# Seeding four LSTM steps at once from 32 stationary columns, with the state in zeroed 32-column tiles

## The chip, the cores and the metric

The kernel runs on one core of a Trainium2 chip. The metric is the device time of one execution in microseconds (us), lower is better; a time is the median of several executions. The profile is one further execution, recorded by the hardware profiler. Engines: PE (TensorE, matmul), with its weight loads shown apart as PEld; DVE (VectorE); ACT (ScalarE); POOL (GpSimd); SP, which issues DMAs.

## The reference, cut to what matters

Two layers on x of shape (8, 512, 256). The part that the change touches is an LSTM over the 512 positions, batch 8, input and state of 256 features; after it come routed attention heads that need all its outputs and their mean over time.

```python
xw = x @ Wx + b                          # (8, 512, 1024), four gates of 256
for t in range(512):
    i, f, o, g = split(xw[:, t] + h @ Wh)    # h: (8, 256)
    c = sigmoid(f) * c + sigmoid(i) * tanh(g)
    h = sigmoid(o) * tanh(c)
```

Step t needs h of step t - 1: the 512 steps are a chain.

## The kernel before, in words

The stages follow each other: a Nystrom attention with an edge sum, the LSTM (`lstm`, lines 598 to 712), routed heads, the second layer's attention, and an RNN with experts. In the LSTM stage the order on PE, ACT and DVE is written out by hand (`manual_schedule`): each engine runs its instructions in the order of the program. POOL and SP are not in that list.

*A step.* The gates' values for all of a step lie in PSUM with the batch on partitions: the 1024 columns are four quarters j of 256, and quarter j goes to partitions 32 j to 32 j + 7, so that each quarter uses its own 32-column tile of PE's array. Of each quarter, 128 columns go to `pgi` (gates i and f), 64 to `pgg`, 64 to `pgo` (function `parts`). For each of these three and each half k of the state, line 677 issues four matmuls, j = 0 to 3, with the state `hp` of 128 x 8 as the stationary operand and a piece of `wh` as the moving one. A float32 matmul appears as two records in the profile, so pgi's 8 matmuls are 16 records.

*The chain.* DVE transposes pgi in 32 x 32 blocks into `G` (line 683), ACT takes tanh (684), the same follows for pgg and pgo (687, 688; the sigmoids are written with tanh, and the weights are scaled for it). DVE forms the products (690, 691) and the new c (693), ACT takes its tanh (695), and DVE writes the state of the step into `ring` (696), a tile of 8 steps. Line 677 of the next step reads it there. X, `to` and `th` are tiles of a pool with three buffers, `ring` of one with two.

*Seeds.* Before its recurrent matmuls, each PSUM tile holds the input share xw + b of its step. `seed` (line 657) puts it there with a matmul of its own: eight columns of the identity, those of the step's batch rows in `xw`, are stationary, and a piece of `xw` is moving. Per step these are 12 matmuls, three per quarter. pgi has two buffers and its seeds for step t + 1 follow the recurrent matmuls of step t directly; pgg and pgo have one, and their seeds stand at the end of step t, after the background pieces, and wait until DVE has transposed the old values.

*Background pieces.* Work that is not part of the chain is cut into generators, of which a step takes a piece after its state is written:
- `project` makes xw for the next 16 steps: two POOL copies, then four matmuls of 128 x 512 moving columns (line 643) and four DVE additions (line 647, 256 columns each), one a step from t % 16 = 7 on: matmuls at 7 to 10, additions at 11 to 14.
- `rest` is the gating of the layer's input, 16 positions at a time in 7 pieces: (1) four matmuls into pv (line 533) and two additions on DVE (535); (2) two ACT operations that read pv (538) and two DVE operations (539); (3) a product (542); (4) a tanh on ACT (544) and, once it is done, a DVE operation (545); (5) a square on ACT (547); (6) a product (549); (7) two additions (552). They stand at t % 16 = 0 to 6.
- `extra` is `adaptive_weights`: 16 rounds of two matmuls with 512 moving columns (line 1065) and an addition with a store (line 1068), at t % 16 = 13 to 15; they end in the first half of the stage.

After each 8 steps DVE sums the ring over time into `hpart` (line 708), and POOL writes half of it to hT, in one instruction (line 709).

Of the kernel before, what the change touches and what calls it, by code (L numbers as in the profile page):

```python
# [18 lines left out]
P = 128  # L19
B = 8  # L20
# [488 lines left out]
def l0_attention(K, es, states):  # L509


    nc, tc, inp = K.nc, K.tc, K.inp
    xT = K.xT
    mm = nc.tensor.matmul
    dp = K.pool(es, "a_d")
    denseT = dp.tile([P, 2, B, S], F32, name="denseT")
    xgT = dp.tile([P, 2, S], F32, name="xgT")
    alpha = dp.tile([P, S], F32, name="alpha")
    wvw = dp.tile([P, 2, D], F32, name="wvw")
    nc.sync.dma_start(out=wvw, in_=inp["wv_w"].rearrange("(k p) n -> p k n", p=P))  # L520

    def gating(gp, pp):


        TT, STT = nc.vector.tensor_tensor, nc.vector.scalar_tensor_tensor
        for t in range(0, S, GT):
            ts = slice(t, t + GT)
            d, x = denseT[:, :, :, ts], xT[:, :, :, ts]
            e, v, sg = [gp.tile([P, 2, B, GT], F32, name=n, tag=n) for n in ("e", "v", "sg")]
            pv = pp.tile([P, 2, B * GT], F32, name="pv", tag="pv")  # L530
            for dc in range(2):
                for k in range(2):
                    mm(pv[:, dc], wvw[:, k, dc * P : (dc + 1) * P], d[:, k], start=(k == 0), stop=(k == 1))
            for dc in range(2):
                TT(e[:, dc], d[:, dc], xgT[:, dc, ts].unsqueeze(1).to_broadcast([P, B, GT]), ALU.add)
            yield
            for dc in range(2):
                nc.scalar.activation(v[:, dc].rearrange("p b t -> p (b t)"), pv[:, dc], AF.Identity, bias=K.cols[:, 2 + dc : 3 + dc])
                STT(x[:, dc], e[:, dc], 2.0, x[:, dc], ALU.mult, ALU.add)
            yield  # L540
            v2, e2, sg2 = [w.rearrange("p k b t -> p (k b) t") for w in (v, e, sg)]
            TT(v2, v2, alpha[:, ts].unsqueeze(1).to_broadcast([P, 16, GT]), ALU.mult)
            yield
            nc.scalar.activation(sg2, v2, AF.Tanh)
            STT(v2, e2, -0.5, v2, ALU.mult, ALU.add)
            yield
            nc.scalar.activation(sg2, sg2, AF.Square, bias=K.ones[:, 0:1], scale=-1.0)
            yield
            TT(v2, v2, sg2, ALU.mult)
            yield  # L550
            for dc in range(2):
                TT(x[:, dc], x[:, dc], v[:, dc], ALU.add)
            yield

    with ExitStack() as e1:
        dr = K.pool(e1, "a_dram", 1, DRAM)
        gp = K.pool(es, "a_g", 2)
        edges = Edges(K, e1, dr)
        with tc.tile_pool(name="n_pre", bufs=1) as pool:
            nystrom(K, modulated(K, pool, dr, denseT), denseT, xgT)  # L560
        hT, lw = states()
        rest = gating(gp, K.pool(es, "a_pv", 1, PSUM))
        with ExitStack() as e2:
            enc0 = K.pool(e2, "a_wv").tile([P, 2, S], F32, name="enc0")
            nc.vector.tensor_tensor(enc0, denseT[:, :, 0, :], xgT, ALU.add)
            with tc.manual_schedule(engines=ORDERED):
                for g, _ in enumerate(edges.sums(enc0, e2, alpha)):
                    if g == 1:
                        weights = lstm_weights(K, lw)
                    if g in (4, 6):  # L570
                        next(rest)
    for _ in range(5):
        next(rest)
    return hT, rest, weights
# [23 lines left out]
def lstm(K, hT, rest, weights, extra):  # L598
# [15 lines left out]
    with ExitStack() as es:  # L614
        wp = K.pool(es, "l_w")
        sp = K.pool(es, "l_s", 3)
        rp = K.pool(es, "l_r", 2)
        xp = K.pool(es, "l_xw", 2)
        psx = K.pool(es, "l_px", 1, PSUM)
        psg = K.pool(es, "l_pg", 1, PSUM)  # L620
        wx, wh, bias = weights
        h0 = wp.tile([P, 2, B], F32, name="h0")
        nc.vector.tensor_scalar(h0, K.h0T, 2.0, None, ALU.mult)
        pick = ident.rearrange("p (b t) -> p t b", b=B)

        pgi = [psg.tile([P, 2, 64], F32, name=f"pgi{i}") for i in range(2)]
        pgg, pgo = [psg.tile([P, 64], F32, name=n) for n in ("pgg", "pgo")]
        for t in (*pgi, pgg, pgo):
            nc.vector.memset(t, 0.0)
        X = sp.tile([P, 4, 2, B], F32, name="X", tag="X")  # L630
        nc.vector.memset(X[:, 3], 0.0)

        def project(t0):

            xw = xp.tile([P, 1024], F32, name="xw", tag="xw")
            px = psx.tile([P, 1024], F32, name="px", tag="px")
            xc = xp.tile([P, 2, P], F32, name="xc", tag="xc")
            for k in range(2):
                nc.gpsimd.tensor_copy(xc[:, k].rearrange("p (b t) -> p b t", b=B), xT[:, k, :, t0 : t0 + XB])
            yield xw  # L640
            for n in range(2):
                for k in range(2):
                    mm(px[:, n * 512 : n * 512 + 512], xc[:, k], wx[:, k, n * 512 : n * 512 + 512], start=(k == 0), stop=(k == 1))
                    yield
            for n in range(4):
                c = slice(n * 256, n * 256 + 256)
                nc.vector.tensor_tensor(xw[:, c], px[:, c], bias[:, c], ALU.add)  # L647
                yield

        def parts(t):  # L650

            return (pgi[t % 2], 0, 128), (pgg, 128, 192), (pgo, 192, 256)

        def seed(t, xw, part):
            for dst, lo, hi in part:
                for j in range(4):
                    mm(dst[32 * j : 32 * j + B], pick[:, t % XB, :], xw[:, j * 256 + lo : j * 256 + hi], start=True, stop=False)  # L657

        proj = project(0)
        xw = next(proj)  # L660
# [1 line left out]
            pass  # L662
        proj = iter(())
        nxt = None
        ring = None
        seed(0, xw, parts(0))
        E = mybir.EngineType
        es.enter_context(K.tc.manual_schedule(engines={E.PE, E.Activation, E.DVE}))
        for t in range(S):
            if t % RB == 0:  # L670
                last = ring
                ring = rp.tile([P, RB, 2, B], F32, name="ring", tag="ring")
            for dst, lo, hi in parts(t):
                for k in range(2):
                    hp = h0[:, k, :] if t == 0 else (ring[:, t % RB - 1, k] if t % RB else last[:, RB - 1, k])
                    for j in range(4):
                        mm(dst[32 * j : 32 * j + B], hp, wh[:, k, j * 256 + lo : j * 256 + hi], start=False, stop=(k == 1))  # L677
            if t + 1 < S:
                if t % XB == XB - 1:
                    xw = nxt  # L680
                seed(t + 1, xw, parts(t + 1)[:1])
            G = sp.tile([P, 4, 2, 32], F32, name="G", tag="G")
            nc.vector.transpose(G[:, 0:2].rearrange("p g k b -> p (g k b)"), pgi[t % 2].rearrange("p g n -> p (g n)"))  # L683
            nc.scalar.activation(X[:, 0:2], G[:, 0:2, :, 0:B], AF.Tanh)  # L684
            to = sp.tile([P, 2, B], F32, name="to", tag="to")
            for g, ps, th in ((2, pgg, X[:, 2]), (3, pgo, to)):
                nc.vector.transpose(G[:, g].rearrange("p k b -> p (k b)"), ps)
                nc.scalar.activation(th, G[:, g, :, 0:B], AF.Tanh)
            pr = sp.tile([P, 2, 2, B], F32, name="pr", tag="pr")
            STT(pr[:, 1], X[:, 1], 1.0, X[:, 3], ALU.add, ALU.mult)  # L690
            STT(pr[:, 0], X[:, 0], 1.0, X[:, 2], ALU.add, ALU.mult)
# [1 line left out]
            STT(X[:, 3], pr[:, 1], 0.5, pr[:, 0], ALU.mult, ALU.add)  # L693
            th = sp.tile([P, 2, B], F32, name="th", tag="th")
            nc.scalar.activation(th, X[:, 3], AF.Tanh, scale=0.5)  # L695
            STT(ring[:, t % RB], to, 1.0, th, ALU.add, ALU.mult)  # L696
            if t % XB == 7 and t - 7 + XB < S:
                proj = project(t - 7 + XB)
                nxt = next(proj)
            next(proj, None)  # L700
            if t % XB < 7:
                next(rest, None)
            if t % XB > 12:
                next(extra, None)
            if t + 1 < S:
                seed(t + 1, xw, parts(t + 1)[1:])
            if t % RB == RB - 1:
                nc.vector.tensor_reduce(K.hpart[:, t // RB], ring.rearrange("p t k b -> p k b t"), AX.X, ALU.add)
                nc.gpsimd.tensor_scalar(
                    hT[:, :, :, t - RB + 1 : t + 1], ring.rearrange("p t k b -> p k b t"), 0.5, None, ALU.mult  # L710
                )
        for _ in extra:
            pass

# [28 lines left out]
def routed_heads(K, hT, T):  # L747
# [4 lines left out]
    with ExitStack() as es:  # L752
# [18 lines left out]
        for k in range(2):  # L771
            mm(pl, hsum[:, k, :], wr[:, k, :], start=(k == 0), stop=(k == 1))
        lg = wp.tile([B, NH], F32, name="lg")
        nc.vector.scalar_tensor_tensor(lg, pl, 0.5 / S, br, ALU.mult, ALU.add)
        nm = wp.tile([B, 1], F32, name="nm")
        sm = wp.tile([B, 1], F32, name="sm")
        nc.vector.tensor_reduce(nm, lg, AX.X, ALU.max, negate=True)
# [272 lines left out]
def adaptive_weights(K, wd, hT):  # L1050
# [2 lines left out]
    mm = nc.tensor.matmul  # L1053
    with ExitStack() as es:
        sp = K.pool(es, "d_s", 2)
        ps = K.pool(es, "d_ps", 1, PSUM)
        for n in range(16):
            c = slice(n * S, (n + 1) * S)
            w2 = sp.tile([P, 2, S], F32, name="w2")
            nc.sync.dma_start(out=w2, in_=inp["ada_w2"][:, c].rearrange("(k p) n -> p k n", p=P))  # L1060
            b2 = sp.tile([B, S], F32, name="b2")
            nc.sync.dma_start(out=b2, in_=inp["ada_b2"][c].partition_broadcast(B))
            pw = ps.tile([B, S], F32, name="pw", tag="ps")
            for k in range(2):
                mm(pw, hT[:, k, :], w2[:, k, :], start=(k == 0), stop=(k == 1))
                yield
# [891 lines left out]
```

## Time and profile before

| | us |
|---|---|
| median of 10 executions (4143.86 to 4151.25) | 4147.59 |
| the profiled execution, its own time | 4140.28 |
| its span, first to last instruction | 4138.5 |
| LSTM stage in it, line 677 first to line 696 last | 457.5 to 1711.6 |

Busy in the whole span: PE 86%, PEld 55%, DVE 58%, ACT 35%, POOL 15%. A line of the costliest groups is read thus: line, engine, operation, what it writes and reads, the shape (128x64 is partitions x elements; "128*8" is the stationary operand), the count, then busy time in us, mean duration in ns, and the idle time of the engine just before with what ended most of it. In a timeline the first column is the start in us, the second the time from the first start to the last end of the instructions that the line merges. Durations of matmuls include their way through the array; how fast they follow each other is seen from their starts.

### The profile page before, as it was taken

The numbers are of one execution on the slowest core, as the hardware profiler recorded it, in microseconds if no ns is written. First come the engines' busy times: TensorE is split into PE (matmuls) and PEld (weight loads), VectorE is DVE, ScalarE is ACT, GpSimd is POOL, SyncE is SP. The second block draws the span as 40 slices with busy tenths as digits, with TensorE's granted clock in tenths as the row PEclk, the third lists the DMA queues.
The fourth block names the chain that finished last, engine by engine and source line by source line (L and its number), as shares of the span: only waits on it lengthen the run. The fifth ranks groups of instructions, "written<-read, shape, count | busy, mean of one in ns | idle before, by whom it ended". The sixth has DMA issues, their size and how long they took to land.

```text
span 4138.5 us, 150218 instructions
## 1 busy us (share of the span) xinstructions
PE 3561.6 (86%) x64484; PEld 2280.7 (55%) x64484; DVE 2396.6 (58%) x8916; ACT 1462.7 (35%) x5391; POOL 605.6 (15%) x1250
## 2 busy tenths in 40 slices
PE   8899888888888888699989899889899798989784
PEld 5533455555555555366545555555555465666563
DVE  4488666666666666466666766766766433333232
ACT  3111233333333333255444444534444222333242
POOL 1010000000000000111022222222222111121312
PEclk9899999999999999899999999999999998999798
DMA  2121000000000000200000000000000302443376
GB/s 104 42 72 67 18 20 15 21 20 15 5 4 4 4 4 17 69 17 24 2 1 1 1 2 1 2 1 1 1 1 1 105 3 94 127 130 107 103 233 212
DMA packets 104844, 173.11 MB, mean 42 GB/s; under 512 B 12576, under 2 KB 71872, under 8 KB 103792
## 3 DMA queue, kind: packets, MB, share of 16 engines
q1 hardware_dynamic: 79792, 114.23, 9.2%
q0 software_dynamic: 12064, 34.34, 2.6%
q10 hardware_dynamic: 12320, 14.94, 1.0%
q8 instruction: 505, 8.27, 0.9%
q14 instruction: 163, 1.34, 0.1%
HBM read 124.53 MB, written 40.10 MB: 40 GB/s over the span
## 4 chain that ended last, share of the span: by engine, by line
PE 43%; DVE 9%; ACT 3%; DMA 2%; issue 2%; SPq 0%; ACTq 0%; POOL 0%; POOLq 0%; DVEq 0%; another core or an unknown queue 0%
PE pg L1375 5%; PE pp L1166 4%; PE pe L1202 4%; DVE sm L1218 3%; PE pt L1241 3%; PE pg L1597 3%; PE po L1257 3%; PE px L1276 3%; PE pe L893 2%; DMA x<-xs 2%; PE pp L869 1%; PE pt L913 1%; PE pv L1186 1%; PE py L1613 1%; PE pg L1359 1%
## 5 line engine op out<-in xcount | busy, mean ns | idle before, releaser
L677 PE MATMUL pgi<-wh,ring 128*8 128x128 f32 x8176 | 319.3, 274 | 214.2 <-DVE ring L696 211.7
L1222 ACT ACTIVATE sm<-sm,nm 128x388 f32<-128x388 f32 (+3 forms) x512 | 283.0, 554 | 345.8 <-DVE nm L1218 345.7
L1380 DVE STREAM_TRANSPOSE ring<-h 128x64 f32<-128x64 f32 x512 | 125.6, 245 | 435.7 <-ACT h L1379 417.6
L684 ACT ACTIVATE X<-G 128x32 f32<-128x32 f32 x512 | 117.1, 229 | 680.2 <-DVE G L683 680.2
L677 PEld LDWEIGHTS pgi<-wh,ring 128*8 128x8 f32 x8176 | 177.2, 89 | 278.4 <-DVE ring L696 277.3
L1241 PE MATMUL pt<-ident,sm 128*128 128x128 f32 x1280 | 214.6, 284 | 104.5 <-ACT eT L1243 55.8
L683 DVE STREAM_TRANSPOSE G<-pgi 128x128 f32<-128x128 f32 x512 | 161.7, 316 | 245.3 <-PE pgi L677 245.3
L1375 PE MATMUL pg<-wh,ring 128*8 128x64 f32 x8176 | 224.8, 232 | 81.2 <-DVE ring L1380 67.8
L1379 ACT ACTIVATE h<-pg 128x64 f32<-128x64 f32 x512 | 114.2, 223 | 494.5 <-PE pg L1375 434.9
L1241 PEld LDWEIGHTS pt<-ident,sm 128*128 128x128 f32 x1280 | 144.2, 141 | 224.7 <-DVE eT L1243 85.7
L1166 PE MATMUL pp<-hn,wqkv 128*128 128x512 f32 x512 | 247.0, 610 | 5.0 <-DVE hn L1151 5.0
L1232 POOL COPY pme<-sm 128x4 f32<-128x4 f32 x512 | 119.5, 233 | 819.8 <-DVE sm L1231 815.5
L1375 PEld LDWEIGHTS pg<-wh,ring 128*8 128x8 f32 x8176 | 124.6, 92 | 193.7 <-DVE ring L1380 152.2
L677 PE MATMUL pgg<-wh,ring 128*8 128x64 f32 x8176 | 208.7, 219 | 1.6 <-issue 1.6
L677 PE MATMUL pgo<-wh,ring 128*8 128x64 f32 x8176 | 209.2, 219 | 0.2
L657 PE MATMUL pgi<-xw,ident 128*8 128x128 f32 x4096 | 207.9, 273 | 0.5 <-DVE xw L647 0.5
L1218 DVE CUSTOM_DVE_ANT_0 sm<-pe,mask 128x260 f32<-128x260 f32 (+2 forms) x384 | 141.7, 425 | 108.5 <-PE pe L1202 104.7
L696 DVE SCALAR_TENSOR_TENSOR ring<-to,th 128x16 f32<-128x16 f32 x512 | 89.7, 175 | 174.5 <-ACT th L695 174.5
L1243 ACT COPY eT<-pt 128x128 f32<-128x128 f32 (+3 forms) x256 | 108.3, 423 | 215.3 <-PE pt L1241 215.2
L1231 DVE TENSOR_SCALAR sm<-sm,rc 128x388 f32<-128x388 f32 (+3 forms) x512 | 177.3, 389 | 9.1
L1597 PE MATMUL pg<-xT,w 128*128 128x128 f32 x992 | 170.6, 297 | 12.7 <-DVE a L1460 8.9
L657 PEld LDWEIGHTS pgg<-xw,ident 128*8 128x8 f32 x4096 | 73.8, 97 | 186.4 <-DVE X L693 93.3
(503 smaller groups left out, 7994.5 us busy)
## 6 DMA issues: line engine op xcount, KB each, us to landing
w<-in_experts_dram SPq DMA_DIRECT2D x124, 384.0 KB
cb<-order POOLq DMA_DIRECT2D x32, 512.0 KB
x<-xs SPq DMA_DIRECT2D x124, 128.0 KB
ys<-y SPq DMA_DIRECT2D x124, 128.0 KB
xs<-zero ACTq DMA_DIRECT2D x2, 4736.0 KB
w<-in_ada_w_dram SPq DMA_DIRECT2D x16, 512.0 KB
w<-in_moh_w_dram SPq DMA_DIRECT2D x32, 192.0 KB
out_dram<-acc SPq DMA_DIRECT2D x32, 128.0 KB
```

Of the source, the lines that this page charges most:

```text
L657: mm(dst[32 * j : 32 * j + B], pick[:, t % XB, :], xw[:, j * 256 + lo : j * 256 + hi], start=True, stop=False)
L677: mm(dst[32 * j : 32 * j + B], hp, wh[:, k, j * 256 + lo : j * 256 + hi], start=False, stop=(k == 1))
L683: nc.vector.transpose(G[:, 0:2].rearrange("p g k b -> p (g k b)"), pgi[t % 2].rearrange("p g n -> p (g n)"))
L1166: mm(pp, T.wqkv[:, k, 0 : 2048].rearrange("p (i g h n) -> p i g h n", i=2, g=4, h=2)[:, i, g, h], self.hn[b][:, k, :], start=(k == 0), sto ...
L1202: mm(pe[a][:, 0 : w - lo], q[r, h, at], k[r, h, lo:w], start=(h == 0), stop=(h == 1))
L1218: nc.vector.tensor_tensor_reduce(out=sm[a][:, lo:w], in0=pe[a][:, 0 : w - lo], in1=T.mask[:, S - n + lo : 4 + S], scale=-1.0 / 8.0, scalar ...
L1222: nc.scalar.activation(sm[a][:, 0:w], sm[a][:, 0:w], AF.Exp, bias=nm[:, a : a + 1], scale=-1.0, accum_out=su[:, a : a + 1])
L1231: nc.vector.tensor_scalar(sm[a][:, 0:w], sm[a][:, 0:w], rc[:, a : a + 1], None, ALU.mult)
L1241: nc.tensor.transpose(pt[:, j, :], sm[a][:, 4 + j * P : 4 + (j + 1) * P], K.ident)
L1375: mm(pg[32 * j : 32 * j + B], hp, M.wh[:, k, 64 * j : 64 * j + 64], start=False, stop=(k == 1))
L1380: M.pace = nc.vector.transpose(M.ring[:, at].rearrange("p k b -> p (k b)"), h)
L1597: mm(pg, W[m][:, k * D + g * P : k * D + (g + 1) * P], X[m][:, k, :], start=(k == 0), stop=(k == 1))
```

## The change

- The PSUM tiles become two sets of pgi, pgg and pgo. A set now holds four consecutive steps (t = 1 to 4, 5 to 8, ...): step t uses rows 8 ((t + 3) % 4) and on of each quarter's 32 partitions. The seeds of a group of four steps are one matmul per quarter and PSUM tile, with 32 identity columns as the stationary operand (`Picks`); where the four steps lie in two projections (the group that begins at t % 16 = 13), they are two matmuls.
- The group's seeds are issued one quarter j per step, during the four steps of the group before, directly after the state is written: three matmuls a step instead of twelve, or six at t % 16 = 9 to 12.
- The state goes into 8 of 32 columns of a ring slot, the other 24 stay zero, and line 677's stationary operand is 128 x 32: the other steps' rows get zero added. The two rings are fixed tiles, zeroed ahead.
- Two shared PSUM banks (`K.px`) serve the gating's pv, the projection's px (now two tiles of 512 columns) and the adaptive weights' pw; each had its own.
- Pieces move: projection from t % 16 = 4 (matmuls at 4, 5, 8, 9; additions at 6, 7, 10, 11); gating at 9 to 15, one piece out of step (2 to 7 at 9 to 14, the next block's 1 at 15), and two pieces a step in steps 0 to 3; adaptive weights at 0 to 2.
- `hpart` is summed from hT instead of the ring, two steps into the next eight; POOL writes hT in four instructions instead of one.

```diff
+        h0 = wp.tile([P, 2, 32], F32, name="h0")
+        rings = [wp.tile([P, RB, 2, 32], F32, name=f"ring{i}") for i in range(2)]
+        banks = [[psg.tile([P, w], F32, name=f"{n}{i}") for n, w in (("pgi", 128), ("pgg", 64), ("pgo", 64))] for i in range(2)]
...
         def parts(t):
-            return (pgi[t % 2], 0, 128), (pgg, 128, 192), (pgo, 192, 256)
-        def seed(t, xw, part):
-            for dst, lo, hi in part:
-                for j in range(4):
-                    mm(dst[32 * j : 32 * j + B], pick[:, t % XB, :], xw[:, j * 256 + lo : j * 256 + hi], start=True, stop=False)
+            return zip(banks[(t + 3) // 4 % 2], (0, 128, 192), (128, 192, 256))
+        def seed(t, j, xw, nxt):
+            for dst, lo, hi in parts(t):
+                at = slice(j * 256 + lo, j * 256 + hi)
+                pick.seed(dst[32 * j : 32 * j + 32], t, xw[:, at], nxt[:, at] if nxt is not None else None)
...
+        for j in range(4):
+            seed(0, j, xw, xw)
+        for j in range(4):
+            seed(1, j, xw, None)
...
-                        mm(dst[32 * j : 32 * j + B], hp, wh[:, k, j * 256 + lo : j * 256 + hi], start=False, stop=(k == 1))
-            if t + 1 < S:
-                if t % XB == XB - 1:
-                    xw = nxt
-                seed(t + 1, xw, parts(t + 1)[:1])
+                        mm(dst[32 * j : 32 * j + 32], hp, wh[:, k, j * 256 + lo : j * 256 + hi], start=False, stop=(k == 1), skip_group_check=True)
...
-            STT(ring[:, t % RB], to, 1.0, th, ALU.add, ALU.mult)
-            if t % XB == 7 and t - 7 + XB < S:
-                proj = project(t - 7 + XB)
+            STT(ring[:, t % RB, :, 8 * (t % 4) : 8 * (t % 4) + 8], to, 1.0, th, ALU.add, ALU.mult)
+            if 0 < t <= S - 4:
+                ahead = (t + 3) // 4 * 4 + 1
+                seed(ahead, (t + 3) % 4, xw, nxt)
+                if t % XB == 12:
+                    xw, nxt = nxt, None
+            if t % XB == 4 and t - 4 + XB < S:
+                proj = project(t - 4 + XB)
                 nxt = next(proj)
             next(proj, None)
-            if t % XB < 7:
+            for _ in range(2 if t < 4 else t % XB > 8):
                 next(rest, None)
-            if t % XB > 12:
+            if t % XB < 3:
                 next(extra, None)
-            if t + 1 < S:
-                seed(t + 1, xw, parts(t + 1)[1:])
+            if t % RB == 2 and t > RB:
+                total(t // RB - 1)
             if t % RB == RB - 1:
-                nc.vector.tensor_reduce(K.hpart[:, t // RB], ring.rearrange("p t k b -> p k b t"), AX.X, ALU.add)
...
+                for i in range(4):
+                    nc.gpsimd.tensor_scalar(
+                        hT[:, :, :, t - RB + 1 + i : t + 1 : 4],
+                        ring[:, i : RB : 4, :, 8 * i : 8 * i + 8].rearrange("p q k b -> p k b q"),
+                        0.5, None, ALU.mult,
+                    )
...
+class Picks:
+    def seed(self, dst, t, xw, nxt):
+        at = t % 16
+        if at == 0:
+            self.mm(dst, self.ends[:, 1], nxt, start=True, stop=False, skip_group_check=True)
+        elif at == 13:
+            self.mm(dst, self.ends[:, 0], xw, start=True, stop=False, skip_group_check=True)
+            if nxt is not None:
+                self.mm(dst, self.ends[:, 1], nxt, start=False, stop=False, skip_group_check=True)
+        else:
+            self.mm(dst, self.steps[:, at : at + 4, :].rearrange("p t b -> p (t b)"), xw, start=True, stop=False, skip_group_check=True)
```

## The prediction

> **What bounds the kernel now.** The change lies in the LSTM stage, so I first cut the execution by stage (busy time of each engine in stretches): the stage runs from 457 to 1712 us, PE is busy 1037 of these 1255 us, DVE 809, ACT 434, and the granted clock is 1.00. 83% busy doesn't say that PE sets the pace, so the next view is who waited for whom, here from 500 to 1700 us (waiter, releaser: us in total, times, longest).
>
> ```profile
> ACT X L684 <- DVE G L683: 641.8, 490, 2.3
> DVE G L683 <- PE pgi L677: 233.0, 475, 1.2
> PE pgi L677 <- DVE ring L696: 203.3, 313, 0.9
> ```
>
> Everybody waits for everybody in turn: a ring of dependences. The timeline of one quiet step (t % 16 = 12; start, length, engine, line, what):
>
> ```profile
> 1348.24 0.17 DVE L696 SCALAR_TENSOR_TENSOR ring<-to,th 128x16 f32<-128x16 f32 x1 [0.34 <-ACT th L695]
> ...
> 1348.47 0.62 PE L677 MATMUL pgi<-wh,ring 128*8 128x128 f32 x16 [0.68 <-DVE ring L696]
> ...
> 1348.91 0.41 PE L677 MATMUL pgg<-wh,ring 128*8 128x64 f32 x16
> ...
> 1349.14 0.41 PE L677 MATMUL pgo<-wh,ring 128*8 128x64 f32 x16
> 1349.17 0.32 DVE L683 STREAM_TRANSPOSE G<-pgi 128x128 f32<-128x128 f32 x1 [0.41 <-PE pgi L677]
> ...
> 1349.36 0.40 PE L657 MATMUL pgi<-xw,ident 128*8 128x128 f32 x8
> ...
> 1350.67 0.18 DVE L696 SCALAR_TENSOR_TENSOR ring<-to,th 128x16 f32<-128x16 f32 x1 [0.34 <-ACT th L695]
> ```
>
> State written, pgi's 16 matmuls, transpose, tanh, three small DVE operations, tanh, state: 2.43 us. PE idles 0.68 us before line 677: in a quiet step the seeds (line 657) lie beside the chain and cost nothing. They cost only where a background piece makes PE late. Here is t % 16 = 8, with a projection piece:
>
> ```profile
> 1339.42 0.40 PE L657 MATMUL pgi<-xw,ident 128*8 128x128 f32 x8
> ...
> 1339.75 1.12 PE L643 MATMUL px<-wx,xc 128*128 128x512 f32 x2
> ...
> 1340.80 0.18 DVE L696 SCALAR_TENSOR_TENSOR ring<-to,th 128x16 f32<-128x16 f32 x1 [0.41 <-ACT th L695]
> 1340.81 0.30 PE L657 MATMUL pgg<-xw,ident 128*8 128x64 f32 x8
> ...
> 1340.93 0.29 PE L657 MATMUL pgo<-xw,ident 128*8 128x64 f32 x8
> ...
> 1341.04 0.29 PE L677 MATMUL pgi<-wh,ring 128*8 128x128 f32 x4
> ```
>
> The last seeds still run when the state is ready. From the ends of line 696, t = 256 to 479, the sixteen steps take, from t % 16 = 0: 2495, 2467, 2426, 2425, three of 2346, 2425, 2572, 2437, 2502, 2505, four of 2425 ns, sum 38.99 us. Without disturbance: 13 x 2425 + 3 x 2346 = 38.56. The other 429 ns are 244 for projection, 42 for gating's matmuls, and 2 x 71 where line 696 starts a new ring tile (idle 0.41 before it, not 0.34: the view of that line lists 62 separate wait instructions). **So the most that freeing PE and this wait can bring is 0.43 x 32 = 13.7 us.** The three short steps are those in which no separate wait stands before ACT's lines 684, 688 and 695 (418 such waits on 512 executions of line 684); they follow the gating's tanh and square, whose spacing the change keeps, so three remain.
>
> **The change, part by part.** *Seeds.* Today's 12 matmuls (24 records) run on four column tiles side by side: 0.22 for pgi, 0.11 for pgg, 0.11 for pgo, 0.44 us. The new 3 matmuls all go to one column tile, j, and can't stand side by side. What that costs is seen once in this trace, ahead of step 0, where the scheduler emitted the seeds quarter by quarter:
>
> ```profile
> 456.24 0.39 PE L657 MATMUL pgi<-xw,ident 128*8 128x128 f32 x2 [0.52 <-DVE xw L647]
> ...
> 456.46 0.28 PE L657 MATMUL pgg<-xw,ident 128*8 128x64 f32 x2
> ...
> 456.57 0.28 PE L657 MATMUL pgi<-xw,ident 128*8 128x128 f32 x1
> 456.58 0.28 PE L657 MATMUL pgo<-xw,ident 128*8 128x64 f32 x2
> ```
>
> 0.22 from pgi to pgg, 0.11 to pgo, pgo as long: one quarter takes 0.44 us, as the four do together. **PE's time for seeds doesn't fall.** At t % 16 = 9 to 12 the group straddles two projections and each seed is two matmuls: 0.88 us.
>
> *PE's own step length.* Recurrent 0.89 (first record to the next kind) + seeds 0.44 + projection 1.17 (gap, two halves of 0.43, load, gap until the next tiled matmul) = 2.51 us as measured today (2507); the order inside changes, not the sum. The chain becomes 2425 + 20 (below) = 2445, so a projection step makes the next late by some 65. The projection's matmuls move to t % 16 = 4, 5, 8 and 9; 9 has the double seeds: 65 + 442 = 507. Together 3 x 65 + 507 = 702 against 244: +458 ns, in 31 groups **+14.2 us**. Gating's matmuls go to 15: PE 2.54 us, +94 against 42 (today the ring's wait of 71 covers part): **+1.6**. Adaptive pieces (to 0, 1, 2) are column-tiled too and take 0.86 without gaps: 0.89 + 0.44 + 0.86 is under 2.445, nothing. Their weights' loads are issued at 446 us, ten before step 0; SP's stores only move.
>
> *Loads of 32 columns for 8.* Not in the trace; nearest are 8 (line 677) and 64 (here lines 255, 64 moving columns, and 928, 128):
>
> ```profile
> 127.07 0.69 PE L255 MATMUL pkv<-v,e3T 128*64 128x64 f32 x16
> ...
> 1764.54 0.85 PEld L928 LDWEIGHTS po<-eT,v 128*64 128x64 f32 x16 [0.76 <-issue]
> ```
>
> Start by start, the first matmul of such a group is 48 to 50 ns longer than the later ones, with 8 columns 4; afterwards line 928's rounds come every 109 ns as line 677's do, and line 255's every 58.5 against 56. So only the first load shows: (49 - 4) x 24/56 = 20 ns a step, **+10.2 us** (ends 0 and 45 ns: 0 and 23 us).
> The Trainium skill (TensorE: Matmul & The Clock Gate, Part 3, The mechanism) says that a load overlaps running matmuls only when its row group differs; here all have all 128 rows, so by it each of pgi's four rounds would show its load, some 4 x 20 = 80 ns a step and 41 us. The 109 ns rounds of line 928 speak against that, and I go by them.
>
> *DVE.* hpart's reduce (0.37, line 708) moves from after step 7 to after step 2 of eight, last in DVE's queue. At t % 16 = 10 it stands behind a projection addition (0.42, line 647) and a gating product (0.42, line 542), and the next transpose behind all three. Such operations follow each other 0.08 before the last one's end: DVE is free some 0.89 after the state, the transpose could start at 0.77: 0.12 x 31 = **+3.7**. At 2 it stands behind line 1068 (0.67), sixteen times, as it did at 15: nothing. The other moved gating pieces meet no second one. The reduce now waits for POOL's copies, three steps old: free.
>
> *The ring's wait.* The ring tiles are no longer handed back, and the reduce over hT, before each reuse, has already waited for POOL: 62 x 0.071 = **-4.4**. If instead each of POOL's four copies were waited for by the state that overwrites it, it would be 256 x 0.071 - 4.4 = +14; I take the first.
>
> *Start, end, rest.* Second group seeded ahead: 4 x 0.33 = +1.3; the ring's memsets, mostly in idle DVE time before 445 us: +0.5 (0 to 1.5); steps 0 to 3 with two gating pieces: the product waits for a tanh, +0.8. After step 511, four POOL copies and then the reduce where one copy (0.64) and a reduce ran beside each other: +0.8. PE's stalls on "issue" in the stage are about 6.7 us (one step alone 1.8); PE has a fifth fewer instructions: -1.5 (0 to -5).
>
> Sum: 14.2 + 1.6 + 10.2 + 3.7 - 4.4 + 2.6 + 0.8 - 1.5 = **+27 us**. On the profiled execution (4140.3, span 4138.5) that is 4167; the runs' median stands 7.3 above it, at 4147.6, which gives **4175**. Its own range, from the ends above, is 4155 to 4192. The measurement can tell about 0.2%, 8.3 us, from no change.
>
> **Rivals.** *Faster: PE is never late.* If a quarter's seeds took a quarter of 0.44, all PE delays and the ring's wait go, and if the wider load is hidden as well: -13.7 + 3.4 = 4137. It decides once the double seeds fit at t % 16 = 9: 2425 - 890 - 1170 = 365 ns, 183 for a single one. Against it: the 0.44 shown ahead of step 0. 5%. *No change: cheap seeds, visible load and DVE queue*: 4137 + 10.2 + 3.7 = 4151. 10%. *Slower still: each round shows its load* (the rule above, or a port shared by four loads): 4175 + 60 ns x 512 = 4206. Against it: line 928. 6%. *Waits*: ACT's second wait in every step, 3 x 79 x 32 = +7.6, or POOL's as priced, +18: 4183 to 4193, 5%; or ACT's second wait gone everywhere, 13 x 79 x 32 = -33: 4142, 2%; for it only that the rearranged pieces may cover it, against it that X, to and th keep three buffers. That the change doesn't do what it says is half of my forecast: fewer seed matmuls, no less PE time. 72% for the forecast.
>
> **Chances and range.** Faster 0.05; same 0.12 (10 + 2); slower 0.83 (72 + 6 + 5). The forecast's own range and the 4151 case make 4151 to 4192.
>
> **What would show it.** In the new profile: line of the recurrent matmuls with a first record some 20 ns longer; the step after t % 16 = 9 longer by half a microsecond, with seeds, then px, then the recurrent matmuls without idle time; the step after 10 longer by 0.1, with the transpose behind a reduce; no separate wait at the state's line; three short steps in sixteen. It is wrong if the seeds of a quarter take 0.11 us, if step 10 starts on time, or if each of pgi's rounds exceeds 109 ns.

## The result, and the profile after

The changed kernel takes 4163.34 us (median, 4158.91 to 4167.02), the kernel before 4146.66 beside it: **ratio 1.0039, 95% interval 1.0030 to 1.0048**, slower by 0.3 to 0.5%. The forecast was 4175 and slower. The sign and the main terms of the mechanism held; the size was 17 us for 27.

Cut by stage first: the profiled executions have spans of 4138.5 and 4159.5, +21.0. That is 4 us more than the medians differ, because the profiled execution of the kernel before lies 6.4 us below its median and that of the changed kernel 2.0. Of the 21.0 +2.4 are there when the LSTM begins (all but a few tenths already at 16 us, ahead of anything that was changed), +19.5 lie in the LSTM (first to last state: 1251.7 and 1271.2), -0.9 after it. In the LSTM PE's records fell from 37416 to 28933, its busy time only from 1037 to 1013 us.

The waits of the changed kernel, 500 to 1700 us (waiter, releaser: us in total, times, longest):

```profile
ACT X L687 <- DVE G L686: 651.6, 483, 1.9
DVE G L686 <- PE pgi L683: 266.9, 410, 1.3
PE pgi L683 <- DVE ring L699: 239.4, 319, 1.2
```

It is the same ring of dependences; each of its three waits is longer, none has gone. The costliest groups (busy time, mean ns, idle time before and what ended it):

```profile
L683 PE MATMUL pgi<-wh,ring 128*32 128x128 f32 x8176 | 330.7, 279 | 259.5 <-DVE ring L699 258.3
L683 PEld LDWEIGHTS pgi<-wh,ring 128*32 128x32 f32 x8176 | 192.8, 109 | 437.5 <-DVE ring L699 412.0
```

The same two lines of the kernel before:

```profile
L677 PE MATMUL pgi<-wh,ring 128*8 128x128 f32 x8176 | 319.3, 274 | 214.2 <-DVE ring L696 211.7
L677 PEld LDWEIGHTS pgi<-wh,ring 128*8 128x8 f32 x8176 | 177.2, 89 | 278.4 <-DVE ring L696 277.3
```

Record by record, only the first of a step is longer (297 for 276 ns). The starts of the four rounds in a step, from the first: 0, 112, 222, 331 ns before and 0, 133, 243, 352 after. The second round is 21 ns late, the later ones keep 109 to 110.

Now the timeline of t = 313 (t % 16 = 9), PE only, then the state of that step on DVE:

```profile
1239.36 0.41 PE L683 MATMUL pgo<-wh,ring 128*32 128x64 f32 x16
1239.59 0.38 PE L747 MATMUL pgi<-xw,ends 128*32 128x128 f32 x2
1239.81 0.38 PE L749 MATMUL pgi<-xw,ends 128*32 128x128 f32 x2
1240.02 0.28 PE L747 MATMUL pgg<-xw,ends 128*32 128x64 f32 x2
...
1240.56 1.13 PE L644 MATMUL px<-wx,xc 128*128 128x512 f32 x2
1241.62 0.32 PE L683 MATMUL pgi<-wh,ring 128*32 128x128 f32 x4
```

```profile
1240.89 0.17 DVE L699 SCALAR_TENSOR_TENSOR ring<-to,th 128x16 f32<-128x16 f32 x1 [0.34 <-ACT th L698]
```

The state is ready at 1241.06, line 683 begins at 1241.62: seeds, then px, then the recurrent matmuls without idle time, half a microsecond late, as forecast. One quarter's seeds take 0.22 + 0.11 + 0.11 = 0.44 us with two records per tile, twice that here.

From the ends of line 699, t = 256 to 479, the sixteen steps take (medians), from t % 16 = 0: 2544, 2445, 2446, 2446, 2446, 2517, 2500, 2446, 2446, 2517, **2941**, 2446, 2366, 2366, 2367, 2446 ns, together 39.69 us for 38.99 (39.72 by the means, in which a few irregular steps count).

### The profile page after: what moved, and what is told of

Same layout as the page of the kernel before. It is cut to its first block, busy times and chain, and to the rows that moved or that the text cites. A ratio compares the mean times of both kernels' runs of the same rounds, so it can differ in the third digit from the quotient of the medians.

```text
span 4159.5 us, 133491 instructions
## 1 busy us (share of the span) xinstructions
PE 3542.5 (85%) x56036; PEld 2381.5 (57%) x56036; DVE 2384.8 (57%) x8919; ACT 1462.3 (35%) x5391; POOL 649.8 (16%) x1442
## 4 chain that ended last, share of the span: by engine, by line
PE 67%; DVE 21%; ACT 5%; issue 3%; DMA 2%; ACTq 0%; SPq 0%; POOL 0%; another core or an unknown queue 0%; POOLq 0%; DVEq 0%
PE pgi L683 7%; PE pg L1410 5%; PE pe L1237 4%; PE pp L1201 4%; PE px L644 3%; DVE sm L1253 3%; DVE G L690 3%; PE pt L1276 3%; PE U L488 3%; PE pg L1632 3%; PE po L1292 3%; PE px L1311 3%; DVE G L686 3%; PE pk L467 3%; ACT th L698 2%
## 5 line engine op out<-in xcount | busy, mean ns | idle before, releaser
L683 PE MATMUL pgi<-wh,ring 128*32 128x128 f32 x8176 | 330.7, 279 | 259.5 <-DVE ring L699 258.3
L683 PEld LDWEIGHTS pgi<-wh,ring 128*32 128x32 f32 x8176 | 192.8, 109 | 437.5 <-DVE ring L699 412.0
L717 POOL TENSOR_SCALAR hT<-ring 128x32 f32<-128x32 f32 x256 | 86.6, 338 | 1160.7 <-DVE ring L699 1160.7
L683 PE MATMUL pgg<-wh,ring 128*32 128x64 f32 x8176 | 208.6, 219 | 0.0
L683 PE MATMUL pgo<-wh,ring 128*32 128x64 f32 x8176 | 208.5, 219 | 0.0
L683 PEld LDWEIGHTS pgg<-wh,ring 128*32 128x32 f32 x8176 | 180.0, 110 | 0.1
```

Of the source, the lines that this page charges most:

```text
L683: mm(dst[32 * j : 32 * j + 32], hp, wh[:, k, j * 256 + lo : j * 256 + hi], start=False, stop=(k == 1), skip_group_check=True)
```

## The experiments

The kernel before took 4100 to 4148 us on the chips used, so each kernel is compared with the kernel before on its own chip. The stage (first to last state) is taken from one profiled execution of each kernel, the sixteen steps are the means of t = 256 to 479 in it. The kernel before was profiled on one chip only, so the stages are all set beside its 1251.7.

| kernel | ratio to before (95%) | stage, us | sixteen steps, us |
|---|---|---|---|
| before | 1 | 1251.7 | 38.99 |
| after | 1.0039 (1.0030 to 1.0048) | 1271.2 | 39.72 |
| wide loads alone | 1.0013 (1.0003 to 1.0023) | 1258.3 | 39.27 |
| hpart from hT alone | 1.0000 (0.9990 to 1.0009) | 1250.5 | 38.98 |
| after, projection apart | 1.0015 (1.0004 to 1.0025) | 1259.8 | 39.27 |
| after, seeds together | 1.0142 (1.0122 to 1.0162) | 1316.4 | 41.21 |
| the same, PE kept busy | 0.9991 (0.9982 to 1.0000) | 1250.0 | 38.95 |
| the same, 17 buffers | 0.9918 (0.9904 to 0.9931) | 1216.5 | 37.88 |
| before, 17 buffers | 0.9936 (0.9922 to 0.9949) | 1229.2 | 38.33 |
| the same, projection in halves | 0.9949 (0.9935 to 0.9962) | 1230.0 | 37.79 |
| the same, hpart from hT, pieces moved | 0.9905 (0.9892 to 0.9919) | 1211.6 | 37.68 |

**Wide loads alone.** Rings and h0 as fixed, zeroed tiles 32 columns wide, nothing else:

```diff
-                        mm(dst[32 * j : 32 * j + B], hp, wh[:, k, j * 256 + lo : j * 256 + hi], start=False, stop=(k == 1))
+                        mm(dst[32 * j : 32 * j + 32], hp, wh[:, k, j * 256 + lo : j * 256 + hi], start=False, stop=(k == 1), skip_group_check=True)
...
-            STT(ring[:, t % RB], to, 1.0, th, ALU.add, ALU.mult)
+            STT(ring[:, t % RB, :, 0:B], to, 1.0, th, ALU.add, ALU.mult)
```

> The kernel before with one part of the change alone: the state stands in 8 of 32 columns of two zeroed ring tiles, and the recurrent matmuls (line 677 of before) take 128 x 32 stationary columns; seeds, pieces and POOL's copy stay as they were. My theory: only the first load of each pgi group shows, some 21 ns a step, 512 x 0.021 = +10.6 us, ratio 1.0026, with a first record of about 297 ns for 272 and rounds that still come every 107 to 109 ns. Rival 1, the load is hidden and the whole loss of the change lies in PE's late steps: ratio 1.000. Rival 2, each of pgi's four rounds shows its load: +41 us, ratio 1.010.

+5.4 us (1.2 to 9.4), by the stage +6.6. The group's line:

```profile
L678 PE MATMUL pgi<-wh,ring 128*32 128x128 f32 x8176 | 327.1, 277 | 214.0 <-DVE ring L697 211.7
L678 PEld LDWEIGHTS pgi<-wh,ring 128*32 128x32 f32 x8176 | 195.8, 109 | 277.6 <-DVE ring L697 277.1
```

First record 297 ns, rounds 133, then 109 to 110: only the first load shows, in each step. The chain's steps are 21 ns longer (2446 for 2425), but those in which PE is late are not (t % 16 = 1 and 8 to 11: 2467, 2575, 2443, 2506, 2506 for 2467, 2571, 2437, 2502, 2505). There PE's own length sets the step, and in it the wider load doesn't show. Alone, by the medians, the load costs 230 ns in sixteen steps (eleven times 21), not 336; the 270 of the table hold one irregular block. Both rivals fall, and the expected ratio of 1.0026 lies above the measured interval for this reason. The rule of the Trainium skill that the prediction weighed (TensorE: Matmul & The Clock Gate, Part 3, The mechanism: a load overlaps only where its row group differs) would have given 80 ns a step; the runs show 21.

**Projection apart**, on the changed kernel:

```diff
-            if t % XB == 4 and t - 4 + XB < S:
-                proj = project(t - 4 + XB)
+            if t == 4 or (t and t % XB == 0 and t + XB < S):
+                proj = project(t - t % XB + XB)
...
-            if t % XB < 3:
+            if t % XB > 12:
                 next(extra, None)
```

> The changed kernel with its projection moved off the steps that carry double seeds: from the second block on its matmuls stand at t % 16 = 0, 1, 4 and 5 (before: 4, 5, 8 and 9), and the adaptive weights' pieces, whose place it takes, at 13 to 15. Same number of instructions. My theory: PE was half a microsecond late in the step after t % 16 = 9 because 0.89 of double seeds and 1.17 of projection stand in one step; apart, each of the four projection steps costs some 70 ns, 4 x 70 = 280 for 692 ns in sixteen steps, 31 x 412 ns = -12.8 us against the changed kernel: about 4150, ratio to before 1.001. Rival, the half microsecond is the projection's or the seeds' own and goes where they go: no change, ratio 1.004.

1.0015 for 1.0039, the stage 11.4 us shorter than after, where 12.8 was expected. t % 16 = 10 takes 2446 for 2941; the steps behind projection matmuls (1, 2, 5, 6) take 2519, 2500, 2513 and 2503. So the loss was the meeting of double seeds and projection. By the sixteen steps the gain is even larger than expected, 39.69 to 39.23 us by the medians, 456 ns for 412. What is missing lies in the stage's last blocks: t = 483 and 485 take 3.79 and 3.94 us, 2.8 us above the usual, the first with a wait of PE on "issue" of 1.2 us and the second at a granted clock of 0.66 (1650 to 1655 us). In the first half of the stage the adaptive weights' pieces at 13 to 15 make t % 16 = 0 take 2625 for 2544, but the step behind it 2442 for 2519: no loss.

**Seeds together.** All four quarters in one step, in the order of the kernel before: for each PSUM tile the four j.

```diff
-            if 0 < t <= S - 4:
-                ahead = (t + 3) // 4 * 4 + 1
-                seed(ahead, (t + 3) % 4, xw, nxt)
+            if t and t % 4 == 0 and t <= S - 4:
+                seed(t + 1, xw, nxt)
```

> The changed kernel with all four quarters of a group's seeds in one step, t % 4 = 0, ordered so that the four column tiles are written by consecutive matmuls; same number of matmuls (12 in one step, 24 at t % 16 = 12, for 3 and 6 in each of four). My theory: the four quarters then lie side by side and take the 0.44 us that one quarter takes alone, so PE's time for seeds falls to a quarter. Steps 5 and 9 no longer carry seeds, 4 and 8 stay late by about 70 ns each: 142 for 692 ns in sixteen steps and nothing for gating's matmuls, some -20 us against the changed kernel, about 4143, ratio to before 0.999. Rival: as in steps 510 and 511 of the changed kernel, which have no seeds and took 3.175 us at a granted clock of 0.50, the idle PE lowers its clock, and each step without seeds or pieces takes up to 0.73 us more, some 200 steps, +146 us, ratio to before about 1.035.

The first half of my theory holds. t = 296, with the seeds of all four quarters:

```profile
1217.44 0.40 PE L742 MATMUL pgi<-xw,steps 128*32 128x128 f32 x8
1217.66 0.29 PE L742 MATMUL pgg<-xw,steps 128*32 128x64 f32 x8
1217.78 0.29 PE L742 MATMUL pgo<-xw,steps 128*32 128x64 f32 x8
1218.00 1.12 PE L644 MATMUL px<-wx,xc 128*128 128x512 f32 x2
```

Eight records follow each other as fast as two did: 0.22 us to pgg, 0.11 to pgo. Four quarters cost PE what one costs. Yet the kernel is the slowest of all, its stage 45 us longer than that of the changed kernel: this is the rival. Steps t = 289 to 293 (stretch, length, busy time and count of PE, PEld, DVE, ACT, POOL, granted clock, DMA share, GB/s):

```profile
1197.23:1199.67 2.44, 1.09 (x48) 0.93 (x48) 1.30 (x7) 0.76 (x4) 0.00 (x0) 1.00 0.00 0
1199.67:1202.12 2.45, 1.09 (x48) 0.93 (x48) 1.31 (x8) 0.77 (x4) 0.00 (x0) 0.86 0.00 0
1202.12:1205.29 3.17, 1.94 (x48) 1.63 (x48) 1.50 (x8) 0.87 (x4) 0.00 (x0) 0.50 0.02 5
1205.29:1208.46 3.17, 3.11 (x73) 2.83 (x74) 1.31 (x7) 0.87 (x4) 0.00 (x0) 0.53 0.00 0
1208.46:1211.59 3.13, 2.89 (x52) 1.23 (x50) 1.30 (x8) 0.76 (x4) 0.32 (x1) 1.00 0.02 5
```

With PE busy for 1.09 of 2.45 us the clock falls in the second such step in a row; each slow step costs 0.73 us. The 0.86 is a mean: cut finer, the clock is 1.00 up to 1201.4 and 0.50 from there to 1208.3. In the LSTM stages of all twelve profiles it is only ever 1.00 or 0.50, and it changes at whole multiples of 3.41 us. It follows the share of such an interval in which PE records are on: of the intervals at 1.00, the 4265 that were followed by another at 1.00 have shares of 0.45 to 1.00, the 54 that were followed by 0.50 have 0.32 to 0.49, so that only between 0.45 and 0.49 both occur. At 0.50, the 52 intervals that brought the clock back have 0.75 to 1.00, the 16 that didn't 0.57 to 0.75. So a row of quiet steps is slowed or not according to where these intervals fall in it.

**The same, PE kept busy.** Seeds are repeated (same values, written anew) in every step without projection or gating matmuls:

```diff
-            if t and t % 4 == 0 and t <= S - 4:
-                seed(t + 1, xw, nxt)
+            if 0 < t <= S - 4 and t % XB not in (4, 5, 8, 9, 15):
+                seed((t + 3) // 4 * 4 + 1, xw, None if t % XB in (10, 11) else nxt)
```

> The kernel of the run with seeds together, but the same four quarters are seeded again in every step that has no projection or gating matmuls (all t % 16 but 4, 5, 8, 9 and 15; each repeat writes the same values anew; at 10 and 11 only the first of the two matmuls). PE then has its 0.44 us of seeds where it would idle and none where it is busy. My theory: the 46 us that seeds together lost against the kernel changed in the ring's projection alone came from the granted clock, which fell to 0.50 after about three steps in a row with PE records on for 1.09 of 2.45 us; with 1.5 us of 2.45 it stays at 1.00, no step is late, and sixteen steps take 13 x 2446 + 3 x 2363 = 38.89 us: 3 us less than before, ratio 0.999. Rival, the seeds in one step disturb in another way (their order on PE, the banks): the slow steps of 3.1 to 3.6 us stay, ratio 1.01.

0.9991 and 38.95 us. Thirteen steps of 2445 to 2449, three of 2363 to 2365 (medians), none late: more work on PE makes the kernel 66 us faster in the stage, because the clock stays at 1.00. Only where the last projection has ended, and steps 4, 5, 8 and 9 have no PE work left, does it fall (t = 502, 506 and 511 take 3.0 to 3.2 us). The one other long step after the first three, t = 484 with 3.96, holds a wait of PE on "issue" of 1.3 us. (The expectation names the kernel compared wrongly: its 46 us are the 45 of the stage against the changed kernel.)

**The last steps.** The changed kernel's end shows the same fall; its last four steps:

```profile
1722.31:1724.75 2.44, 1.53 (x54) 1.37 (x54) 1.30 (x7) 0.77 (x4) 0.00 (x0) 1.00 0.00 0
1724.75:1727.19 2.44, 1.09 (x48) 0.93 (x48) 1.30 (x8) 0.76 (x4) 0.32 (x1) 0.94 0.02 7
1727.19:1730.37 3.18, 1.93 (x48) 1.61 (x48) 1.31 (x8) 0.88 (x4) 0.32 (x1) 0.50 0.00 0
1730.37:1733.54 3.17, 1.94 (x48) 1.63 (x48) 1.31 (x7) 0.87 (x4) 0.32 (x1) 0.50 0.00 0
```

The test seeds on to the end, into the free set of banks; it was run once, for its profile:

```diff
-            if 0 < t <= S - 4:
+            if 0 < t:
...
-                    xw, nxt = nxt, None
+                    xw, nxt = nxt or xw, None
```

> The changed kernel with seeds also in its last three steps (for a group that is never used, from the last projection, into the set of banks that is free). My theory: steps 510 and 511 took 3.175 us each because the granted clock fell to 0.50 once the seeds had ended; here it stays at 1.00 and both take 2446 ns, 1.46 us less, which only the profile can show. Rival, the last steps are slow for what follows them (adaptive pieces, the heads' loads): 3.175 us again.

Steps 510 and 511 take 2450 and 2446 ns, at this clock:

```profile
1726.00:1728.00 2.00, 1.47 (x54) 1.31 (x54) 1.13 (x6) 0.63 (x4) 0.31 (x1) 1.00 0.00 0
1728.00:1730.80 2.80, 1.53 (x54) 1.36 (x54) 1.48 (x8) 0.91 (x5) 0.32 (x1) 1.00 0.02 6
```

**hpart from hT alone**, on the kernel before:

```diff
+            if t % RB == 2 and t > RB:
+                total(t // RB - 1)
             if t % RB == RB - 1:
-                nc.vector.tensor_reduce(K.hpart[:, t // RB], ring.rearrange("p t k b -> p k b t"), AX.X, ALU.add)
```

> The kernel before with one part of the change alone: hpart is summed from hT, two steps into the next eight, instead of from the ring; POOL's copy stays one instruction. My theory: the reduce then waits for POOL where nothing is late, the state needs no wait of its own, and the 71 ns at each eighth step go: up to 62 x 0.071 = -4.4 us, less where gating's matmuls hold the same step up (0.042 of it at t % 16 = 0, -1.3 us), so -3 to -4.4, ratio 0.9990. The reduce itself costs nothing at t % 16 = 2 and 10, as after. Rival, it stands before the transpose and costs 0.12 at one or both places: ratio 1.000 to 1.001.

A miss: ratio 1.0000. The wait is gone (no wait instruction at the state's line), t % 16 = 0 and 8 are some 70 ns shorter (2425, 2504 for 2496, 2571), and the steps behind them longer by as much (2537, 2505 for 2467, 2437). t = 304, with gating's matmuls, on PE and then on DVE:

```profile
1203.33 0.62 PE L680 MATMUL pgi<-wh,ring 128*8 128x128 f32 x16 [0.68 <-DVE ring L699]
...
1204.55 1.16 PE L533 MATMUL pv<-denseT,wvw 128*128 128x128 f32 x8
...
1205.87 0.40 PE L680 MATMUL pgi<-wh,ring 128*8 128x128 f32 x7
```

```profile
1205.53 0.18 DVE L699 SCALAR_TENSOR_TENSOR ring<-to,th 128x16 f32<-128x16 f32 x1 [0.34 <-ACT th L698]
```

PE needs 2.54 us from one step's first matmul to the next's, whenever the state comes; an earlier state only waits longer for it. The reduce itself costs nothing in either place.

**ACT's own wait.** The kernel before with more buffers for X, G, to, pr and th:

```diff
-        sp = K.pool(es, "l_s", 3)
+        sp = K.pool(es, "l_s", 17)
```

> The kernel before with 17 buffers for three of the small tiles of a step (X, G, to, pr and th share the pool, which had 3). My theory of the three short steps in sixteen: they are those in which ACT needs no wait instruction of its own before its first tanh; it needs one because it overwrites a buffer that was used three steps ago. With 17 buffers the waits go in the other 13 steps as well: 32 x 13 x 79 ns = -33 us, about 4114, ratio 0.992, and about 10 separate waits at line 684 for 418. Rival, the short steps are short for another reason (the pieces on DVE and ACT in them): ratio 1.000, whether the waits go or not.

```profile
L684 ACT ACTIVATE X<-G x512: 228/228/231, 459.8 to 1689.0; 128x32 f32<-128x32 f32 x171
L684 ACTq EVENT_SEMAPHORE  x15: 17/17/38, 449.0 to 1688.9; - x15
```

This is the view of one line; the second row lists its separate wait instructions, 15 of them. The same row of the kernel before:

```profile
L684 ACTq EVENT_SEMAPHORE  x418: 17/17/38, 447.4 to 1710.3; - x140
```

All undisturbed steps take 2342 to 2344, about what the three short ones took (2346): ratio 0.9936, by it -26 us (the stage is 22.5 us shorter). Not -33, because the steps in which PE is late (1 and 8 to 11) stay at 2466, 2575, 2434, 2504 and 2503.

**The same on the kernel with PE kept busy** (again only the line above).

> The same with 17 buffers for X, G, to, pr and th. If both causes are right, neither PE nor ACT's separate wait lengthens a step: 16 x 2363 = 37.81 us in sixteen steps, -38 us against the kernel before, about 4064, ratio 0.991, faster than both kernels and than the kernel before with 17 buffers (sixteen steps of 38.33 us there). Rival, with shorter steps PE or DVE becomes late at the projection: between 0.991 and 0.994.

0.9918; sixteen steps of 2362 to 2367 each. Without the late steps, the buffers now bring the full 13 x 82 ns.

**Projection in halves**, on the kernel before with 17 buffers:

```diff
-            for n in range(2):
-                for k in range(2):
-                    mm(px[:, n * 512 : n * 512 + 512], xc[:, k], wx[:, k, n * 512 : n * 512 + 512], start=(k == 0), stop=(k == 1))
-                    yield
             for n in range(4):
                 c = slice(n * 256, n * 256 + 256)
-                nc.vector.tensor_tensor(xw[:, c], px[:, c], bias[:, c], ALU.add)
-                yield
+                for k in range(2):
+                    mm(px[:, c], xc[:, k], wx[:, k, c], start=(k == 0), stop=(k == 1))
+                    if k == 1:
+                        nc.vector.tensor_tensor(xw[:, c], px[:, c], bias[:, c], ALU.add)
+                    yield
```

> The kernel before, 8 stationary columns and its seeds as they were, with 17 buffers and with the projection cut finer: eight steps (t % 16 = 7 to 14) with one matmul of 256 columns each for four with 512, each second one with its addition. My theory: PE's step was 0.89 + 0.44 + 1.17 = 2.50; with half a matmul 0.89 + 0.44 + some 0.7 = 2.06, never late. Sixteen steps of 2342, plus 124 that stay at t % 16 = 1 (gating's matmuls) and 2 x 71 for the ring's wait: 37.74 us, -40 us against before, about 4062, ratio 0.990. Rival, the gaps around a full-array matmul are the cost and come twice as often: 0.9936, as with 17 buffers alone.

A miss in the time (0.9949), a hit in the second half of the stage: 37.79 us. In the first half the projection now reaches to t % 16 = 14 and meets the adaptive weights' matmuls at 13 and 14; steps 14 and 15 take 2930 and 2908 ns, sixteen times. So, with those pieces at 2 to 4 and hpart summed from hT:

```diff
-            if t % XB > 12:
+            if 1 < t % XB < 5:
                 next(extra, None)
```

> The kernel before, 8 stationary columns, with 17 buffers for X, G, to, pr and th, the projection in eight halves (one matmul of 256 columns at t % 16 = 7 to 14), hpart summed from hT, and the adaptive weights' pieces at t % 16 = 2 to 4 instead of 13 to 15, where they met the projection's last halves and made steps 14 and 15 take 2.93 and 2.91 us in the first half of the stage (sixteen times 1.15 us, 18 us). My theory: fifteen steps of 2343 and one of 2465 at t % 16 = 1: 37.6 us in sixteen in both halves, -44 us in the stage against before, ratio 0.989, the fastest kernel of all. Rival, the adaptive matmuls make PE late wherever they stand: the first half stays 0.6 to 1.2 us longer in sixteen steps, ratio 0.992 to 0.995.

**0.9905, the fastest kernel here**, 4064 for 4100 us. Fifteen steps of 2342 to 2346 and one of 2537 (2465 had been expected) in both halves; the rival falls. 0.989 was expected; of the missing 6 us a stall of PE at t = 493 (6.94 us for that step, 3.05 for the next) takes 5. The next section tells what such stalls are.

## Why the prediction was right, and where its size was off

| step | forecast, us | measured, us | from |
|---|---|---|---|
| projection and double seeds | +14.2 | +13.9 | excess 71 + 54 + 71 + 496 = 692 ns for 244, 31 groups |
| gating's matmuls | +1.6 | +1.7 | 99 for 42 ns |
| wider loads | +10.2 | +10.6 | 2446 for 2425 |
| DVE's reduce | +3.7 | 0 | below |
| the ring's wait | -4.4 | -4.4, in this account | 71 twice in sixteen steps |
| start | +2.6 | +1.1 | steps 1 to 3 |
| end | +0.8 | +0.6 | last steps +1.5, after them -0.9 |
| irregular steps (forecast as PE's stalls on "issue") | -1.5 | -4.0 | what single steps take above the usual of their place, about 6.5 before, 2.5 after |
| sum | +27.2 | +19.5 | the profiled pair from the first state to its end: 18.6 |

*Right, and shown by experiment.* One quarter's seeds take as long as four quarters' (seeds together); the loss sits where double seeds meet the projection (apart); the wider load shows once a step (wide loads alone). These make 24 of the 27 us. The wider load was sized from far rows, of 64 columns, and came out within 4%. The three short steps remained, with 421 separate waits for 418, and their cause is now tested (17 buffers). The sum of +19.5 misses the 18.6 of the profiled pair by 0.9; these rows are good to about that.

*DVE's reduce, 0 for +3.7.* The step that failed: "the next transpose behind all three", ready 0.12 late. The order in DVE's queue is as forecast; the timeline of t = 314 on DVE:

```profile
1243.84 0.17 DVE L699 SCALAR_TENSOR_TENSOR ring<-to,th 128x16 f32<-128x16 f32 x1 [0.34 <-ACT th L698]
1243.93 0.42 DVE L648 TENSOR_TENSOR xw<-px,bias 128x256 f32<-128x256 f32 x1
...
1244.26 0.41 DVE L542 TENSOR_TENSOR v<-v,alpha 128x256 f32<-128x256 f32 x1
...
1244.59 0.28 DVE L652 TENSOR_REDUCE hpart<-hT 128x16 f32<-128x128 f32 x1
...
1244.79 0.31 DVE L686 STREAM_TRANSPOSE G<-pgi 128x128 f32<-128x128 f32 x1
```

I had priced the reduce at 0.37, its time over the ring; over hT, where the summed positions lie next to each other, it takes 0.28. With that the forecast's own working gives 0.80 for 0.89, some 1 us in place of 3.7. The transpose began 0.78 after the state, where by the forecast pgi alone would let it begin at 0.77, and the step behind takes 2446 ns, like an undisturbed one. The sign that was named for this term, a step behind t % 16 = 10 that is 0.1 us longer, didn't come.

*The ring's wait.* Booked as a gain of its own it was wrong, though the sum was not: the run with hpart from hT shows that before, taking this wait away gives nothing, since PE was late in the next step anyway. The 244 and 42 ns charged to PE were net of it. Of +14.2 + 1.6 - 4.4 only the sum, 11.4, has a meaning; measured 11.2.

*Start and end.* The second group's seeds cost nothing before step 0 (+1.3 forecast), the rings' memsets and the copies ahead of line 498 some 0.3 us (+0.5). The seeds do end later, 1.05 us behind the last xw addition for 0.29, but with px as two tiles these additions end 0.8 us sooner after the projection's first matmul (7.25 us for 8.04). Steps 1 to 3, with adaptive weights' and gating pieces in them, take 1.1 us more than usual (+0.8 forecast). The end held a cost I hadn't seen: without seeds, steps 510 and 511 lose 1.46 us to the clock. It is small here by luck: the design spreads the seeds over all steps for another reason, and so keeps PE busy enough. Put together, they cost 45 us.

*Irregular steps, -4.0 for -1.5*, inside the range given (0 to -5), but this row holds more than what the forecast named: PE's waits on "issue" alone are 2.5 us before and 0.2 after by the view of waits. Some of the rest is the lower clock behind a stall; the other irregular steps weren't followed up. The greatest stall lies where the next stage's loads start. Before, then after, in the columns of the stretches above:

```profile
1655.00:1660.00 5.00, 4.87 (x163) 3.06 (x162) 2.57 (x14) 1.50 (x8) 0.00 (x0) 1.00 1.00 372
1660.00:1665.00 5.00, 2.47 (x80) 1.82 (x84) 2.15 (x10) 1.09 (x5) 0.00 (x0) 0.83 0.99 381
```

```profile
1660.00:1665.00 5.00, 3.97 (x110) 3.00 (x110) 2.85 (x16) 1.56 (x9) 0.00 (x0) 1.00 0.96 391
```

With the DMA engines busy throughout, PE of the kernel before waited 1.6 us at once for nothing that these views name, and its clock fell on top (0.83 is the mean of the stretch, 0.50 from 1663.3 to 1666.7): t = 492 took 4.22 us. The changed kernel went through the same burst with a wait of 0.2. What PE waited for can be told from the packets that the trace holds beside the instructions. The queue of instructions (q8 on the page) brought 505 packets of 16 KB in the kernel before, one for each 256 of PE's 129258 records, and 439 for 112391 in the changed one. All 36 waits of PE on "issue" of 0.15 us or more in the LSTM stages of the twelve profiles stand at the same place in a block of 256 records (193 or 194 records past a multiple of 256), and each ends 1.20 to 1.61 us after such a packet has landed. So PE had run out of instructions. Why the packet came late wasn't tried. A busy DMA isn't needed for it, since 25 of the 36, all but one of them under 0.9 us, lie where the DMA share is 0.14 or less; but ten of the eleven over 1 us lie in the burst.

## What to carry to other kernels

Matmuls on four column tiles are paid for once when the tiles take turns, so count PE's time by rounds, not by instructions: spreading a group over steps, one tile each, cost what four had cost together. A wait on the chain and an engine that is late in the next step are one loss, not two; undo either alone and ask what sets the step then. And before chasing a change's few nanoseconds, look at the step that nothing disturbs: its 79 ns of separate waits for buffers were worth more (-26 us) than everything that the change was about (+17).

## What the runs showed of the hardware that was not expected

- The granted clock falls although PE is never idle for long. With bursts of 1.09 us and idle gaps of 1.35 us (PE's longest wait in those steps: 1.36) its mean was 1.00 in the first step, 0.86 in the second and 0.50 in the third; with 1.53 of 2.45 us busy it stayed at 1.00 (steps 505 to 508 of the changed kernel, and all filled steps). Interval by interval of 3.41 us, it fell after busy shares of 0.32 to 0.49 and held after 0.45 and more. The Trainium skill (TensorE: Matmul & The Clock Gate, Part 1, HAM oscillation) asks for no idle gaps above some 3.4 us; gaps of 1.35 us were enough here, where they came in each step.
- At a clock of 0.50 a step takes 3175 ns for 2446, only 30% more, since most of the ring of dependences isn't PE.
- A stationary operand of 32 columns for 8 costs 21 ns at the first load after an idle PE and nothing at the loads that follow (rounds of 109 to 110 ns either way).
- PE's waits on "issue" in this stage stand at one and the same place in each 256 of its instructions and end 1.20 to 1.61 us after the 16 KB packet of instructions has landed. The longest lie where the DMA share is 0.98 to 1.00, in the stage's last blocks: 1.6 us in the kernel before, 2.8 in the fastest one, where the clock then fell to 0.50 and one step took 6.94 us.
